# A graph-attention kernel: the last softmax of a layer spread over the next pass, two more products behind the last scores, the bias row on ScalarE

## The chip, the cores and the metric

The kernel runs on one core of a Trainium2 chip. The metric is the device time of one execution in microseconds; the time before is 2698.18 us, the median of three runs (2697.36 to 2700.32). A core has TensorE (PE: matmuls into PSUM banks; PEld is its weight load), VectorE (DVE), ScalarE (ACT), GpSimd (POOL) and SyncE (SP), which issues most of the DMAs. Each runs its own instructions in order and waits on semaphores for the others.

## The reference

Everything is float32. The input is x [128, 64, 768] and a symmetric adjacency of zeros and ones [128, 64, 64] with a full diagonal. After a first normalization there are two layers (l = 0, 1):

```python
h = maximum(layernorm(x), 0)
for l in range(2):
    u_left  = einsum('bih,bjh->bij', h, h @ W_left[l].T)  / sqrt(768)
    u_right = einsum('bih,bjh->bij', h, h @ W_right[l].T) / sqrt(768)
    u = u_left on and above the diagonal, u_right below it (where adj is 1)
    e = exp(u) * adj
    attention = e / (sum(e, axis=2) + 1e-10)
    h = relu(layer_norm(attention @ (h @ W_lin[l].T + b_lin[l])))   # ddof 1, eps added to sigma
x + h
```

## The kernel before, in words

Each layer has two passes. **Pass one** computes the scores and the attention. The 32 parts of 256 tokens are taken in 11 groups (`SUPER`): one of two parts and ten of three. For a group the kernel multiplies weight forms with sums of tokens (a fast matrix multiplication with 40 products, `PRODUCTS`, in place of 54 block products); DVE and ACT read each product out of its PSUM bank and add it into the operands m0, m1, m2 (L847, L851, and L245 for plain additions). The products go round four banks of C, D, X, Y, Z, V. POOL makes the token sums (L245). The scores of a group are 288 small matmuls (L676) into the banks `sc`; they stand four products into the next group. The softmax of a group, a Python generator `chain` (L680 to L715), is cut into eight steps by `yield`: POOL multiplies the two triangles of the adjacency into `wm`; DVE multiplies the scores into `wm` (L690), adds the two halves (L694); ACT takes Exp (L696); DVE masks and sums (L698, L700), divides (L702 to L704), transposes (L708); SP stores the attention with eight DMAs (L713). The steps are put into slots of the next group; a slot is half a product (`put_all`, `turn_of`, `run`), and what a slot holds is issued there on whatever engine it is for.

The last group has no next group. After its 40 products (and the flush of all slots left) come products 0 and 1 of pass two (`LEAD`), then the scores of the last group, then all eight softmax steps in one piece. The adjacency, `wm` and the operands lie in a pool that ends with pass one; its space is used by the tiles of pass two. The 51 places `g` of 128 x 512 elements live through the whole kernel and are handed out and taken back in order through the queue `free`.

During the last group of pass one the plan of `final_of` also loads and prepares what pass two needs: the weights of the linear map (ACT centres them, L233 and L237; DVE and POOL by turns make 17 sums of them), the token sums of its first block (POOL), and the bias row (`bias`, L885 to L913): three DMAs of 256 columns, copied to all partitions, then, on DVE, the sum over the row, the centring, two additions and two negations.

**Pass two** goes over 16 blocks of 512 tokens. `linear` (L1154) does 15 products per block in the order of `ORDER`, each of eight matmuls (L934). Its second entry is the bank by a name that `NAME` maps to the physical bank; `FIRST` tells which products take a fresh bank and `PRELOAD` which of these are first filled with a piece of the bias row by an ACT copy (L923: products 0, 3, 5 and 9). Counted from 0, the banks are 0 in Z, 1 in V, 2 in Z, 3 in X, 4 in Z, 5 in Y, 6 in Z, 7 in X, 8 in Z. The first use of an output piece in `hl` is an ACT activation (L300), later ones are DVE additions (L245); a bank is free for the next product when it is read. Then come the attention times `hl` (L976 or L999), the normalization and the stores.

The order of the work is written by hand: the instructions of an engine stand in the order in which the Python code issues them.

Of the kernel before, what the change touches and what calls it, by code (L numbers as in the profile page):

```python
# [10 lines left out]
F32 = mybir.dt.float32  # L11
I32 = mybir.dt.int32
AF = mybir.ActivationFunctionType
ALU = mybir.AluOpType
# [3 lines left out]
def kernel(  # L18
# [12 lines left out]
    nc = tc.nc  # L31
    B, S, H = x.shape
    L = w_lin.shape[0]
    P = 128
# [35 lines left out]
    def put_all(slot, fs, step=1):  # L70
        for f in fs:
            if f is not None:
                put(slot, f)
            slot += step
        return slot
# [245 lines left out]
    KEEP = {}  # L321
# [299 lines left out]
    def pass_one(l, start, final):  # L621
        with tc.tile_pool(name=f"one{l}", bufs=2, reuse_waits="tile") as sp, \
# [41 lines left out]
                return M[v][:, i * K2:(i + 1) * K2, :, k, :]  # L664

            def scores(k):
                adj, nq = ADJ[k], 2 * len(SUPER[k])
                p = KEEP["scores"].rearrange("p a (q m) -> p (a q) m", m=P)
                for q in range(nq):
                    ht, m = HT[1, l, SUPER[k][q // 2]], M[q // 2]  # L670
                    for c in range(C):
                        for h in range(PAIR):
                            b = q % 2 * PAIR + h
                            mb = m[:, c, b].rearrange("p k j -> p (k j)")
                            for e in (0, 32):
                                nc.tensor.matmul(p[h * S + e:h * S + e + 32, q, e:e + 95],  # L676
                                                 ht[:, c, b * S + e:b * S + e + 32], mb[:, e:e + 95],
                                                 start=(c == 0), stop=(c == C - 1))

                def chain():  # L680

                    wm = sp.tile([P, 6, 2, S], F32, name="wm", bufs=1)[:, :nq]
                    for n in range(2):
                        nc.gpsimd.tensor_tensor(wm[:, :, n], adj[:, :nq, 1 - n],
                                                tri[:, n].unsqueeze(1).to_broadcast([P, nq, S]), op=ALU.mult)
                    yield
                    flat = wm.rearrange("p q k j -> p (q k j)")
                    for i in range(0, P, 32):
                        r = wm.rearrange("p q k j -> p q (k j)")[i:i + 32, :, i % S:i % S + 95]
                        nc.vector.tensor_tensor(r, p[i:i + 32, :nq, i % S:i % S + 95], r, op=ALU.mult)  # L690
                        if i % S:
                            yield
                    v = adj[:, :nq, 0, :]
                    nc.vector.tensor_add(v, wm[:, :, 0], wm[:, :, 1])  # L694
                    yield
                    nc.scalar.activation(v, v, AF.Exp, scale=ISTEMPER if k == 0 else ISTEMPER / 4)  # L696
                    yield
                    nc.vector.tensor_mul(v, v, adj[:, :nq, 1, :])  # L698
                    s = stat.tile([P, 6], F32, name="s", bufs=2)[:, :nq]
                    nc.vector.reduce_sum(s, v, axis=mybir.AxisListType.X)  # L700
                    yield
                    nc.vector.tensor_scalar_add(s, s, EPS_ATT)  # L702
                    nc.vector.reciprocal(s, s)
                    nc.vector.tensor_tensor(v, v, s.unsqueeze(2).to_broadcast([P, nq, S]), op=ALU.mult)  # L704
                    yield

                    at = flat[:, :nq * S].rearrange("p (g q i) -> p g q i", g=2, q=nq)
                    nc.vector.transpose(at.rearrange("p g q i -> p q g i"),  # L708
                                        v.rearrange("p q (g j) -> p q g j", g=2))
                    to = ATT[l][k].rearrange("(b g j) q (h i) -> b h g j q i", b=2, g=2, h=2)  # L710
                    for a in range(4):
                        for g in range(2):
                            nc.sync.dma_start(to[a // 2, a % 2, g], at[a * 32:(a + 1) * 32, g])  # L713

                CHAIN[k] = chain()  # L715

            def softmax(k):
                return [lambda: next(CHAIN[k], None)] * 8

            mid = None  # L720
# [148 lines left out]
            for n in sorted(plan):  # L869
                for f in plan.pop(n):  # L870
                    f()
            for i in range(2):
                LEAD[i] = fresh(l, i, (0, 1))
                multiply(l, 0, i, LEAD[i], (0, 1))
            scores(last)
            for f in softmax(last):
                f()

    rows = {}

# [4 lines left out]
    def bias(l):  # L885


        ab = [free.popleft() for _ in range(2)]
        W[l, "bias"] = ab
        t = rows["bias", l] = [ab[n // 2][:, n % 2, :] for n in range(4)]  # L890
        todo = [lambda i=i, to=to: row(f"b{i}", b_lin[l], i * D, (i + 1) * D, t[to]) for i, to in enumerate((1, 2, 0))]
        bm = stat.tile([P, 3], F32, name="bm", bufs=1)

        bs = stat.tile([P, 1], F32, name="bs", bufs=1)

        def mean():
            for n in range(3):
                nc.vector.reduce_sum(bm[:, n:n + 1], t[n], axis=mybir.AxisListType.X)
            nc.vector.reduce_sum(bs, bm, axis=mybir.AxisListType.X)

        def centred():
            nc.vector.tensor_scalar_mul(bs, bs, -1.0 / H)
            for n in range(3):
                nc.vector.tensor_scalar_add(t[n], t[n], bs)

        def combined():
            nc.vector.tensor_add(t[1], t[1], t[0])
            nc.vector.tensor_add(t[3], t[1], t[2])

        def negated(n):  # L910
            nc.vector.tensor_scalar_mul(t[n], t[n], -1.0)

        return todo, [mean, centred, combined, lambda: negated(0), lambda: negated(2)]  # L913

    AHEAD = []
    PRELOAD = {0: 0, 3: 1, 5: 2, 9: 3}
# [1 line left out]
    def fresh(l, i, rs):  # L918

        bank = ps_st.tile([P, 2 * TH], F32, name=NAME[FIRST[i][0]])  # L920
        b = bank.rearrange("p (r d) -> p r d", r=2)[:, :len(rs)]
        if i in PRELOAD:
            nc.scalar.copy(b, rows["bias", l][PRELOAD[i]].unsqueeze(1).to_broadcast([P, len(rs), D]))  # L923
        return b
# [4 lines left out]
    def multiply(l, u, i, p, rs, between=None):  # L929
        s, _, t, _ = ORDER[i]  # L930
        b, w = tokens_of((2, l, u)), W[l, "n"]
        for n, r in enumerate(rs):
            for c in range(K2):
                nc.tensor.matmul(p[:, n], b[t][:, c, r * P:(r + 1) * P], w[s][:, c, :],  # L934
                                 start=(i in FIRST and i not in PRELOAD and n == c == 0),
                                 stop=(c == K2 - 1), skip_group_check=True)
            if n == 0 and between:
                between()

    def pass_two(l, aside):  # L940
        last = l == L - 1
        with tc.tile_pool(name=f"two{l}", bufs=2, reuse_waits="tile") as sp, \
# [211 lines left out]
            def linear(u, rs, base, ends, more):  # L1154

                if rs[0] == 0:
                    HL[u] = sp.tile([P, Q, H], F32, name="hl", bufs=2)
                hl, seen = HL[u], set()
                bank = {} if LEAD else {"X": AHEAD.pop()}
                early = {0: 3, 2: 5, 6: 9}  # L1160
                for i, (s, at, t, _) in enumerate(ORDER):
                    if i in LEAD:
                        p = bank[at] = LEAD.pop(i)
                        run(base + 2 * i)
                    else:
                        if i in FIRST and i not in PRELOAD:
                            bank[at] = fresh(l, i, rs)
                        p = bank[at]
                        multiply(l, u, i, p, rs, lambda: run(base + 2 * i))
                    read(p, lambda o: hl[:, o % 2 * 2 + rs[0]:o % 2 * 2 + rs[0] + len(rs), o // 2 * D:(o // 2 + 1) * D],  # L1170
                         i, seen, nc.vector if (len(rs), rs[0], i) == (1, 0, 2) and not last else nc.scalar)
                    if i in early:
                        bank[FIRST[early[i]][0]] = fresh(l, early[i], rs)
                    if i == 11 and more and 12 not in ends:
                        AHEAD.append(fresh(l, 0, more))
                    if rs[-1] and t in TS[2, l, u]:
                        free.append(TS[2, l, u].pop(t))
                    if i in ends:
                        what, slots = ends[i]
                        if slots:  # L1180
                            for f, n in zip(finish(*what), slots):
                                put(n, f)
                        else:
                            finish_block(what, more)
                    run(base + 2 * i + 1)
# [100 lines left out]
```

## Time and profile before

| what | value |
|---|---|
| median of the runs | 2698.18 us (2697.36 to 2700.32) |
| profiled execution, whole | 2704.83 us |
| its span from first to last instruction | 2701.9 us |
| mean granted clock of TensorE | 0.988 |
| end of pass one, layer 0 and layer 1 | near 881 to 894 and 2207 to 2219 us |

A line of the timeline has the start in us, the duration, the engine, the source line, the operation, the output and input tiles, their shapes and a count; rows of the same kind that follow each other are merged. In brackets stands how long the engine was idle before it and what released it. "128x512 f32 x3" is three instructions of 128 partitions by 512 elements. PEclk is the granted clock of TensorE as a share of full speed. Ends of matmuls are modelled: a row of eight lasts 1.89 us while the next one starts some 1.73 us after it. SPq and ACTq rows are DMAs being issued. A group line gives the least, the median and the longest duration in ns.

### The profile page before, as it was taken

To read this page: it belongs to the slowest core of one execution; us is meant where nothing else is said; L and a number is where in the kernel's file an instruction comes from. 1 tells how busy PE (TensorE), PEld (TensorE's weight loads), DVE (VectorE), ACT (ScalarE), POOL (GpSimd) and SP (SyncE) were. 2 spreads that over 40 slices of the span, in tenths; PEclk is the share of its full clock that TensorE was granted. 3 is DMA by queue.
4 is the path that set the end of the run, shared out by engine and by line. 5 is a ranking of instruction groups with operands and counts; after the bars stand their busy time and mean duration, and the time that the engine had idled before them with its cause. 6 is when DMAs were issued, how large, how long until landed. Compare 5 with 4: busy or idle time off the path is not lost. (4 is left out here: it accounts for less than half of the span.)

```text
span 2701.9 us, 46786 instructions
## 1 busy us (share of the span) xinstructions
PE 2615.5 (97%) x18042; PEld 2229.1 (83%) x18042; DVE 1765.2 (65%) x2800; ACT 925.8 (34%) x1941; POOL 1725.6 (64%) x1326
## 2 busy tenths in 40 slices
PE   9889999999999899999899999999999979999998
PEld 8778888888887788888678888888888868888886
DVE  7868868776778445554424766776766685666667
ACT  5512222222213144445452212222222315455543
POOL 4756757666667547766215666676666666787786
PEclk9999999999999999999999999999999999999999
DMA  7353443334321344446786443353442105655655
GB/s 215 81 138 80 115 102 92 86 91 123 80 68 62 120 129 155 144 152 205 210 232 181 104 111 86 85 121 91 115 114 68 64 12 156 183 158 159 180 160 149
DMA packets 263358, 336.52 MB, mean 125 GB/s; under 512 B 56290, under 2 KB 195298, under 8 KB 263138
## 3 DMA queue, kind: packets, MB, share of 16 engines
q1 hardware_dynamic: 246338, 325.28, 44.0%
q10 hardware_dynamic: 16800, 8.26, 1.1%
q8 instruction: 144, 2.36, 0.4%
q14 instruction: 76, 0.62, 0.1%
HBM read 218.11 MB, written 115.34 MB: 123 GB/s over the span
## 5 line engine op out<-in xcount | busy, mean ns | idle before, releaser
L245 POOL TENSOR_TENSOR g<-ht 128x512 f32<-128x512 f32 x584 | 769.1, 1327 | 523.6 <-ACT ht L377 135.4
L245 POOL TENSOR_TENSOR g<-g,g 128x512 f32<-128x512 f32 x295 | 378.8, 1292 | 139.9 <-DVE g L245 42.6
L245 POOL TENSOR_TENSOR g<-ht,g 128x512 f32<-128x512 f32 x256 | 339.9, 1335 | 154.7 <-PE X L654 40.3
L934 PE MATMUL Z<-g,g 128*128 128x256 f32 x1024 | 248.5, 385 | 18.3 <-ACT hl L300 9.8
L654 PE MATMUL C<-g,g 128*128 128x256 f32 x1008 | 243.3, 385 | 15.3 <-DVE m L245 7.7
L654 PE MATMUL X<-g,g 128*128 128x256 f32 x1008 | 241.0, 382 | 9.3 <-ACT m L828 4.1
L934 PEld LDWEIGHTS Z<-g,g 128*128 128x128 f32 x1024 | 194.4, 193 | 50.8 <-issue 12.0
L654 PEld LDWEIGHTS C<-g,g 128*128 128x128 f32 x1008 | 191.8, 192 | 46.7 <-POOL g L245 9.4
L654 PEld LDWEIGHTS X<-g,g 128*128 128x128 f32 x1008 | 191.4, 191 | 38.4 <-issue 4.9
L654 PE MATMUL Y<-g,g 128*128 128x256 f32 x912 | 216.5, 380 | 0.0
L654 PE MATMUL D<-g,g 128*128 128x256 f32 x880 | 208.4, 380 | 4.8 <-issue 2.8
L654 PE MATMUL Z<-g,g 128*128 128x256 f32 x864 | 204.7, 380 | 0.0
L377 ACT ACTIVATE ht<-ht,b_col,a_col 128x256 f32<-128x256 f32 x384 | 195.2, 591 | 24.1 <-DMA ht<-h 20.3
L245 DVE TENSOR_TENSOR m<-m,D 128x512 f32<-128x512 f32 x180 | 118.5, 679 | 116.1 <-ACT m L847 98.3
L654 PEld LDWEIGHTS Y<-g,g 128*128 128x128 f32 x912 | 174.2, 191 | 24.0
L654 PEld LDWEIGHTS D<-g,g 128*128 128x128 f32 x880 | 167.0, 190 | 29.1 <-issue 3.7
L934 PE MATMUL X<-g,g 128*128 128x256 f32 x768 | 185.6, 384 | 0.0
L654 PEld LDWEIGHTS Z<-g,g 128*128 128x128 f32 x864 | 163.5, 190 | 23.3 <-issue 0.5
L654 PE MATMUL V<-g,g 128*128 128x256 f32 x768 | 181.4, 379 | 0.0
L934 PEld LDWEIGHTS X<-g,g 128*128 128x128 f32 x768 | 148.3, 193 | 21.5 <-issue 0.6
L245 DVE TENSOR_TENSOR hl<-hl,Y 128x512 f32<-128x512 f32 (+1 forms) x136 | 89.0, 654 | 115.4 <-PE Y L934 96.6
L1134 POOL TENSOR_TENSOR z<-z,b 128x768 f32<-128x768 f32 x62 | 112.6, 1828 | 78.5 <-DVE z L1131 77.2
(215 smaller groups left out, 4728.9 us busy)
## 6 DMA issues: line engine op xcount, KB each, us to landing
ht<-h SPq DMA_DIRECT2D x126, 768.0 KB, 6.4
h<-xb SPq DMA_DIRECT2D x124, 384.0 KB, 5.9
z<-z SPq DMA_DIRECT2D x128, 192.0 KB, 3.1
x<-z SPq DMA_DIRECT2D x128, 192.0 KB, 5.4
xr<-in_x_dram SPq DMA_DIRECT2D x120, 192.0 KB, 3.8
out_dram<-xr SPq DMA_DIRECT2D x120, 192.0 KB, 2.7
x<-in_x_dram SPq DMA_DIRECT2D x112, 192.0 KB, 5.6
g<-form SPq DMA_DIRECT2D x40, 256.0 KB, 5.1
```

The costliest lines, as they stand in the source:

```text
L245: (eng.tensor_add if sign == "+" else eng.tensor_sub)(o, a, b)
L377: nc.scalar.activation(ht, ht, AF.Relu, bias=cols[1][:, c:c + 1], scale=cols[0][:, c:c + 1])
L654: nc.tensor.matmul(p[:, g], w[:, c, g * P:(g + 1) * P], t[:, c, :], start=(new and g == c == 0), stop=(c == K2 - 1), skip_group_check=True)
L934: nc.tensor.matmul(p[:, n], b[t][:, c, r * P:(r + 1) * P], w[s][:, c, :], start=(i in FIRST and i not in PRELOAD and n == c == 0), stop=(c ...
L1134: nc.gpsimd.tensor_add(zs[k], zs[k], rows["b"])
```

## The change

Three things are changed, in both layers.

1. The softmax generator moves out of `scores`, so that it can begin ahead of the scores. For the last group it borrows three places `g` from `free`: one for a copy of the mask (a new POOL instruction), one for the values, one for the transposed result. Nothing of it but `wm`, up to the addition of the two halves, lies in the pool of pass one. Its first step (POOL) is issued ahead of products 0 and 1, the next three (DVE) behind the products that follow the scores, and the last four go into slots 6, 9, 12 and 15 of pass two's first block; then the places go back.
2. Besides products 0 and 1, pass two's products 3 and 5 are issued ahead of pass two: their banks are filled in front of the scores, their matmuls stand behind the scores. `linear` no longer asks for their banks.
3. The bias row's sums (an activation that also gives the sum), its centring and its negations go to ACT; DVE keeps the sum of the three sums, its scaling and the two additions. There are six steps of four slots in place of five.

```diff
             def scores(k):
-                adj, nq = ADJ[k], 2 * len(SUPER[k])
+                nq = 2 * len(SUPER[k])
...
-                CHAIN[k] = chain()
+            def chain(k):
+                adj, nq = ADJ[k], 2 * len(SUPER[k])
+                p = KEEP["scores"].rearrange("p a (q m) -> p (a q) m", m=P)
+
+                spare = [free.popleft() for _ in range(3)] if k == last else ()
+                own = [t.rearrange("p c d -> p (c d)")[:, :nq * S] for t in spare]
...
+                mask = adj[:, :nq, 1, :]
+                if own:
+                    mask = own[0].rearrange("p (q j) -> p q j", q=nq)
+                    nc.gpsimd.tensor_copy(mask, adj[:, :nq, 1, :])
+                yield
...
+                v = own[1].rearrange("p (q j) -> p q j", q=nq) if own else adj[:, :nq, 0, :]
+                nc.vector.tensor_add(v, wm[:, :, 0], wm[:, :, 1])
...
+                nc.vector.tensor_mul(v, v, mask)
...
+                at = (own[2] if own else flat[:, :nq * S]).rearrange("p (g q i) -> p g q i", g=2, q=nq)
...
+                free.extend(spare)
 
             def softmax(k):
+                CHAIN[k] = chain(k)
                 return [lambda: next(CHAIN[k], None)] * 8
...
-            for i in range(2):
+            steps = softmax(last)
+            steps[0]()
+            for i in (0, 1, 3, 5):
                 LEAD[i] = fresh(l, i, (0, 1))
+                if i < 2:
+                    multiply(l, 0, i, LEAD[i], (0, 1))
+            scores(last)
+            for i in (3, 5):
                 multiply(l, 0, i, LEAD[i], (0, 1))
-            scores(last)
-            for f in softmax(last):
+            for f in steps[1:4]:
                 f()
+            put_all(6, steps[4:], 3)
...
+        def sums():
+            for n in range(3):
+                nc.scalar.activation(t[n], t[n], AF.Copy, accum_out=bm[:, n:n + 1])
+
         def mean():
+            nc.vector.reduce_sum(bs, bm, axis=mybir.AxisListType.X)
+            nc.vector.tensor_scalar_mul(bs, bs, -1.0 / H)
+
+        def centred():
             for n in range(3):
-                nc.vector.reduce_sum(bm[:, n:n + 1], t[n], axis=mybir.AxisListType.X)
-            nc.vector.reduce_sum(bs, bm, axis=mybir.AxisListType.X)
-
-        def centred():
-            nc.vector.tensor_scalar_mul(bs, bs, -1.0 / H)
-            for n in range(3):
-                nc.vector.tensor_scalar_add(t[n], t[n], bs)
+                nc.scalar.activation(t[n], t[n], AF.Identity, bias=bs)
...
         def negated(n):
-            nc.vector.tensor_scalar_mul(t[n], t[n], -1.0)
+            nc.scalar.activation(t[n], t[n], AF.Copy, scale=-1.0)
 
-        return todo, [mean, centred, combined, lambda: negated(0), lambda: negated(2)]
+        return todo, [sums, mean, centred, combined, lambda: negated(0), lambda: negated(2)]
...
-                    if i in early:
+                    if i in early and early[i] not in LEAD:
                         bank[FIRST[early[i]][0]] = fresh(l, early[i], rs)
```

More of the change, by code (lines that the diff above doesn't have):

```diff
@@ L678, in scores @@
                                                  start=(c == 0), stop=(c == C - 1))
[L680 to L713, printed above, removed]
@@ L715, in scores @@
-                CHAIN[k] = chain()
+            def chain(k):
[3 more added lines that the diff above has]
+                own = [t.rearrange("p c d -> p (c d)")[:, :nq * S] for t in spare]
+                wm = sp.tile([P, 6, 2, S], F32, name="wm", bufs=1)[:, :nq]
+                for n in range(2):
+                    nc.gpsimd.tensor_tensor(wm[:, :, n], adj[:, :nq, 1 - n],
+                                            tri[:, n].unsqueeze(1).to_broadcast([P, nq, S]), op=ALU.mult)
+                mask = adj[:, :nq, 1, :]
[3 more added lines that the diff above has]
+                yield
+                flat = wm.rearrange("p q k j -> p (q k j)")
+                for i in range(0, P, 32):
+                    r = wm.rearrange("p q k j -> p q (k j)")[i:i + 32, :, i % S:i % S + 95]
+                    nc.vector.tensor_tensor(r, p[i:i + 32, :nq, i % S:i % S + 95], r, op=ALU.mult)
+                    if i % S:
+                        yield
+                v = own[1].rearrange("p (q j) -> p q j", q=nq) if own else adj[:, :nq, 0, :]
+                nc.vector.tensor_add(v, wm[:, :, 0], wm[:, :, 1])
+                yield
+                nc.scalar.activation(v, v, AF.Exp, scale=ISTEMPER if k == 0 else ISTEMPER / 4)
+                yield
+                nc.vector.tensor_mul(v, v, mask)
+                s = stat.tile([P, 6], F32, name="s", bufs=2)[:, :nq]
+                nc.vector.reduce_sum(s, v, axis=mybir.AxisListType.X)
+                yield
+                nc.vector.tensor_scalar_add(s, s, EPS_ATT)
+                nc.vector.reciprocal(s, s)
+                nc.vector.tensor_tensor(v, v, s.unsqueeze(2).to_broadcast([P, nq, S]), op=ALU.mult)
+                yield
+                at = (own[2] if own else flat[:, :nq * S]).rearrange("p (g q i) -> p g q i", g=2, q=nq)
+                nc.vector.transpose(at.rearrange("p g q i -> p q g i"),
+                                    v.rearrange("p q (g j) -> p q g j", g=2))
+                to = ATT[l][k].rearrange("(b g j) q (h i) -> b h g j q i", b=2, g=2, h=2)
+                for a in range(4):
+                    for g in range(2):
+                        nc.sync.dma_start(to[a // 2, a % 2, g], at[a * 32:(a + 1) * 32, g])
+                free.extend(spare)
```

## The prediction

> **What bounds the kernel now.** I read the page first, then the order of time around the two places where pass one hands over to pass two, then the granted clock there, then the waits of TensorE.
>
> ```profile
> span 2701.9 us, 46786 instructions
> PE 2615.5 (97%) x18042; PEld 2229.1 (83%) x18042; DVE 1765.2 (65%) x2800; ACT 925.8 (34%) x1941; POOL 1725.6 (64%) x1326
> ```
>
> TensorE (PE) is busy 97% of the span, so only its holes, and stretches in which it is slow, can be won. The largest hole that the change touches is the end of pass one. This is layer 0, in order of time (start, duration, engine; in brackets the idle time before it and who ended it):
>
> ```profile
> 885.96 6.20 PE L676 MATMUL sc<-m,ht 128*32 128x95 f32 x265 [1.15 <-DVE m L245]
> 893.79 3.03 DVE L690 TENSOR_TENSOR wm<-sc,wm 32x570 f32<-32x570 f32 x4 [4.91 <-issue]
> 896.86 0.56 DVE L694 TENSOR_TENSOR adj<-wm 128x384 f32<-128x384 f32 x1
> 897.45 0.52 ACT L696 ACTIVATE adj<-adj 128x384 f32<-128x384 f32 x1 [20.16 <-DVE adj L694]
> 897.88 0.58 ACT L300 ACTIVATE hl<-Z 128x512 f32<-128x512 f32 x1
> 898.61 3.75 PE L934 MATMUL Z<-g,g 128*128 128x256 f32 x8 [4.92 <-ACT hl L300]
> 902.15 3.12 PE L934 MATMUL X<-g,g 128*128 128x256 f32 x8
> 902.39 0.60 ACT L300 ACTIVATE hl<-Z 128x512 f32<-128x512 f32 x1 [2.93 <-PE Z L934]
> 905.11 1.89 PE L934 MATMUL Z<-g,ht 128*128 128x256 f32 x8
> ...
> 910.29 1.89 PE L934 MATMUL X<-g,g 128*128 128x256 f32 x8
> ```
> ```profile
> core 0: us, PE busy (x) PEld busy (x) DVE busy (x) ACT busy (x) POOL busy (x), PEclk, DMA share, GB/s
> 899.00:902.00 3.00, 3.00 (x8) 2.37 (x8) 2.34 (x6) 0.47 (x1) 0.00 (x0) 0.50 0.02 5
> 906.00:912.00 6.00, 6.00 (x29) 5.30 (x28) 0.76 (x2) 1.68 (x3) 0.33 (x1) 1.00 0.82 265
> ```
>
> The scores end at 893.8, when VectorE (DVE) starts on them. Product 2 of pass two reuses bank Z, whose read stands on ScalarE (ACT) behind the softmax's Exp, and Exp waits for DVE: a hole of 4.92 us. Then products 2 and 3 run at a granted clock of 0.50. Counting the products of pass two as they stand in the kernel's table, the five products 2, 3, 4, 5, 6 lie between 893.79 and the start of product 7 at 910.29: 16.50 us. At full clock a product takes (910.29-905.11)/3 = 1.727 us, five take 8.63; 7.9 us are lost. Layer 1 has the same hole, and the scores of an earlier group show that the scores themselves leave the clock alone:
>
> ```profile
> 2211.71 6.97 PE L676 MATMUL sc<-m,ht 128*32 128x95 f32 x288 [1.15 <-DVE m L245]
> 2223.59 3.75 PE L934 MATMUL Z<-g,g 128*128 128x256 f32 x8 [4.90 <-ACT hl L300]
> ...
> 2234.97 1.89 PE L934 MATMUL X<-g,g 128*128 128x256 f32 x8
> ```
> ```profile
> 809.38 1.47 PE L676 MATMUL sc<-m,ht 128*32 128x95 f32 x58 [0.34 <-issue]
> 810.78 1.99 PE L654 MATMUL C<-g,g 128*128 128x256 f32 x8
> ```
> ```profile
> 2165.99 1.99 PE L654 MATMUL C<-g,g 128*128 128x256 f32 x8 [3.45 <-POOL g L245]
> ```
>
> A product straight behind scores takes 1.99 us, not 3.75, and even 3.45 us of idleness left the next product at 1.99. So it is the 4.9 us hole that halves the clock.
>
> **Part A: two more products behind the scores, the softmax's tail spread.** The instruction order of the changed program shows PE going scores, 3, 5, 2, 4, 6, 7. ACT gets the bias copies for banks X and Y in front of the reads of products 0, 1 and 2; Exp follows the read of 2, the other softmax steps stand between DVE's reads of pass two.
>
> Products 3 and 5 need banks X and Y. DVE's last reads of these lie before 888.9 (it is idle for 4.91 us until 893.79), so both copies are done while the scores run; ACT, idle for 20.16 us there, has the room. The reads of 0 and 1 can run then too. In layer 1 the output tile of these reads lies over the score operands, so they may wait for the scores' end; two reads of 0.6 us are over long before product 2, 3.5 us later. PE therefore goes on at 893.8 without a hole, at full clock.
>
> What is late next: 2, 4 and 6 all use bank Z and now follow each other directly, so PE waits twice for ACT's read of Z. Price from the rows: the read starts 0.03 us after product 2's modelled end (898.61+3.75 = 902.36, read at 902.39), takes 0.60, and PE starts 0.15 us after a read's end (897.88+0.58 to 898.61): 0.78. Rows last 0.16 longer than their spacing, so a turn costs 0.95 us; two cost 1.9. Bounds: nothing, if ACT were ahead, and the clock case below. New stretch: 8.63 + 1.9 = 10.5 us in place of 16.50 in layer 0 (gain 6.0) and of 2234.97-2218.68 = 16.29 in layer 1 (gain 5.8). **Sum 11.7 us.**
>
> Exp now stands in front of ACT's reads of products 4 and 6, and PE waits for those. Its turn comes at 893.8 + 3 x 1.727 + 0.6 = 899.6; DVE's sum of the scores is ready at 896.86+0.56 = 897.42, so there are 2.2 us of slack. On DVE the softmax's 0.55 us steps push its reads of X and Y back by about 1 us; banks X and Y are next written by 7 and by the copy for 9, several products later, so that costs nothing, and 1:1 if those came sooner.
>
> **Part B: the bias row on ScalarE.** In the last group of pass one DVE is behind. PE's rows (first and last of the stretch, and the long waits), DVE's bias row work, and what ACT does then:
>
> ```profile
> 843.04 1.99 PE L654 MATMUL D<-g,g 128*128 128x256 f32 x8 [0.91 <-POOL g L245]
> 845.12 1.07 DVE L898 TENSOR_REDUCE bm<-g 128x1 f32<-128x256 f32 x3 [0.36 <-DMA g<-in_b_lin_dram]
> 848.99 3.72 DVE L904 TENSOR_SCALAR g<-g,bs 128x256 f32<-128x256 f32 x3
> 854.02 1.59 PEld L654 LDWEIGHTS X<-g,g 128*128 128x128 f32 x8 [2.31 <-POOL g L245]
> 854.06 1.97 PE L654 MATMUL X<-g,g 128*128 128x256 f32 x8 [1.93 <-DVE m L245]
> 858.01 1.99 PE L654 MATMUL C<-g,g 128*128 128x256 f32 x8 [0.26 <-DVE m L245]
> 858.59 0.60 ACT L847 ACTIVATE m<-D 128x512 f32<-128x512 f32 x1 [19.25 <-DVE m L851]
> 861.42 1.35 DVE L911 TENSOR_SCALAR g<-g 128x256 f32<-128x256 f32 x1
> 863.42 1.99 PE L654 MATMUL X<-g,g 128*128 128x256 f32 x8 [1.47 <-DVE m L851]
> 865.84 1.27 POOL L245 TENSOR_TENSOR g<-g,g 128x512 f32<-128x512 f32 x1 [3.22 <-DVE g L245]
> 867.30 1.96 PE L654 MATMUL C<-g,g 128*128 128x256 f32 x8
> ```
> ```profile
> 2168.89 1.99 PE L654 MATMUL D<-g,g 128*128 128x256 f32 x8 [0.91 <-POOL g L245]
> ...
> 2193.06 1.97 PE L654 MATMUL C<-g,g 128*128 128x256 f32 x8
> ```
>
> From 843.04 to 867.30 lie eleven products; at 1.727 they take 19.0 us, so 5.3 us are lost (layer 1: 24.17, so 5.2). DVE is rid of 1.07+3.72+1.35 = 6.1 us per layer (and of one short negation), more than the whole loss, so it stops being late. GpSimd (POOL) remains: at 854.02 it released the weights at the same moment as DVE its bank, and it waits 3.22 us for DVE itself. Bounds per layer: 5.3, and 1.7 (0.26+1.47, the waits that are DVE's alone). I take 4.5, near the upper end, because POOL's own longest wait in that stretch is for the same late DVE and goes with it; some tenths stay where POOL is the later one. **Sum 9.0 us.**
>
> ```profile
> L233 ACT ACTIVATE g<-g x36: 399/407/416, 815.0 to 2161.7; 128x256 f32<-128x256 f32 x36
> L233 ACT ACTIVATION_READ_ACCUMULATOR g<-g x36: 186/192/203, 815.3 to 2162.0; 128x1 f32 x36
> L237 ACT ACTIVATE g<-g,wmm x36: 491/494/512, 822.7 to 2166.1; 128x256 f32<-128x256 f32 x36
> 837.00 0.61 ACTq L641 DMA_DIRECT2D adj<-in_adj_dram  x1
> 881.18 1.96 POOL L684 TENSOR_TENSOR wm<-adj,tri 128x384 f32<-128x384 f32 x2
> 911.67 1.27 POOL L245 TENSOR_TENSOR g<-ht 128x512 f32<-128x512 f32 x1 [28.52 <-DMA ht<-h]
> ```
>
> ACT takes on 3 x (0.41+0.19) + 3 x 0.49 + 2 x 0.41 = 4.1 us per layer, inside its 19.25 us of idleness; without that cover 4.1 us would come back. The sums wait for the third row's load (about 845, by DVE's wait on it) and hold ACT's queue; behind them stand the four adjacency loads, now issued near 847 and not at 837. POOL needs them at 881: over 30 us of slack. The row's finish sits one step of four slots later, at slot 60 of about 80.
>
> **Part C: borrowed places and queues.** The mask copy adds one POOL instruction per layer, some 1 us by the 881.18 row (two in 1.96), in front of 28.52 us of idleness: nothing, 1 us without it. Three places are out of the pool until slot 15 and come back at its end. On SP the eight stores of the last softmax move behind the next block's two loads and the two attention loads; those go out sooner, since they need only the scores' end, and POOL, which waited 28.52 us for one, starts sooner. The loads of the block after that stand behind the stores, as before; their users are a block (some 28 us) away. Nothing on PE's path.
>
> **Sum:** 11.7 + 9.0 = 20.7 us off the profiled execution (span 2701.9, 2704.83 with what lies around it, 6.65 above the median 2698.18 of the runs shown). I take the gain to be the same in the undisturbed runs: 2698.2 - 20.7 = **2677.5 us**.
>
> **Rivals.**
> 1. POOL, not DVE, bounds the end of pass one: its weight release at 854.02 speaks for it, its own waits for DVE against. B gives nothing: 2686.5.
> 2. The turns on bank Z hold the clock down: products 2, 4 and 6 go at the halved spacing of 902.15-898.61 = 3.54 instead of 1.727, 5.4 us per layer, A shrinks to 0.8: 2688.4. The 3.45 us row at full clock speaks against it. The Trainium skill's page "TensorE: Matmul & The Clock Gate", section "A second HAM failure mode: psum-queue depth-cycling", says that frequent short pauses of PE between bank groups can make the gate fall and rise again; by that rule this rival is what would happen. No row here shows it.
> 3. The change does not do what it says: products 3 and 5 find X or Y still held, wait for the copies until the softmax is through, and DVE's relief only uncovers POOL: about 2696, within 0.2%. The DVE idle before 893.79 speaks against it.
> 4. Slower: Exp late on ACT. If DVE's sum into a borrowed place had to wait for that place's last reader, Exp would hold ACT's reads of Z, and PE with it, 1:1 beyond the 2.2 us of slack. To end over 5.4 us slower it must be late by 2.2 + (20.7+5.4)/2 = 15.3 us in each layer; at 16 us the time is 2698.2 - 20.7 + 2 x 13.8 = 2705. The places taken are those longest free, which speaks against it.
>
> **How the numbers follow.** 0.2% (5.4 us) is about what a measurement of this kernel can tell from no change. Forecast 0.74, rival 1 0.10, rival 2 0.06, rival 3 0.05, rival 4 0.05. Faster 0.90, within 0.2% 0.05, slower 0.05. Low end: turns free (3.8 more) and all of B (1.5 more): 2672. High end: it takes in rivals 1 and 2: 2689. The forecast's own range, with B between 1.7 and 5.3 per layer, is 2672 to 2683.
>
> **What would show it.** Right: no idle row before the product behind the scores, clock 1.00 there, two waits of about 0.8 us on ACT's read of Z, about 10.5 us from scores' end to product 7; eleven products in some 20 us in the last group; no DVE work on the bias row but the small mean and two additions. Wrong: a halved clock with only short pauses, waits on POOL in place of DVE, Exp starting after 900, or stalls of PE in the second block of pass two.

## The result and the profile after: half of the forecast gain

The changed kernel takes 2687.55 us (median of 8 runs, 2684.21 to 2692.35), the kernel before 2698.86 us beside it (8 runs, 2697.36 to 2706.13). The medians differ by 11.3 us; the ratio of the runs is 0.9961, with an interval of 0.9952 to 0.9970, which is 10.5 us, between 8 and 13. The forecast was 2677.5 us, a gain of 20.7 us. The direction was right. The time lies inside the wide range, 2672 to 2689, which took in two rivals, but outside the forecast's own, 2672 to 2683, and the gain is half of what was worked out.

The first lines of the page after:

```profile
span 2685.4 us, 46818 instructions
PE 2610.8 (97%) x18042; PEld 2225.0 (83%) x18042; DVE 1756.3 (65%) x2784; ACT 933.0 (35%) x1963; POOL 1727.2 (64%) x1328
```

The profiled execution took 2688.04 us, its span is 16.5 us shorter than that of before. Not all of that is the change's: the product into bank D that opens the prediction's stretch stood at 843.04 and now stands at 839.00, so 4.0 us were there before any changed instruction mattered. The same product stood at 840.90 in a run of the kernel before with one added store behind this place (below), so such an offset comes from one execution to the next.

**The end of pass one, layer 1, is as forecast.** The changed kernel's order of time there (columns as before: start, duration, engine, line, operation, count, in brackets the idle time and who ended it):

```profile
2200.65 5.81 PE L676 MATMUL sc<-m,ht 128*32 128x95 f32 x248 [1.15 <-DVE m L245]
...
2204.33 1.83 SPq L366 DMA_DIRECT2D ht<-h  x2
...
2206.75 1.02 PE L676 MATMUL sc<-m,ht 128*32 128x95 f32 x40 [0.29 <-issue]
...
2207.71 1.99 PE L950 MATMUL X<-g,g 128*128 128x256 f32 x8
...
2213.84 1.99 PE L950 MATMUL Z<-g,ht 128*128 128x256 f32 x8 [0.69 <-ACT hl L300]
...
2216.62 1.97 PE L950 MATMUL Z<-g,g 128*128 128x256 f32 x8 [0.78 <-ACT hl L300]
...
2218.42 1.89 PE L950 MATMUL X<-g,g 128*128 128x256 f32 x8
```

Product 3 follows the scores without a hole, at full clock (1.99). Products 4 and 6 wait 0.69 and 0.78 us for bank Z. From product 3 to product 7 it takes 2218.42 - 2207.71 = 10.7 us, where 10.5 were forecast. From the start of the scores to product 7 it was 2234.97 - 2211.71 = 23.26 us and is 17.77: a gain of 5.5.

**Layer 0 gains only 2.4** (24.33 us before, 902.11 - 880.15 = 21.96 after). The order of time and the stretches of the changed kernel:

```profile
880.15 6.20 PE L676 MATMUL sc<-m,ht 128*32 128x95 f32 x265 [1.15 <-DVE m L245]
...
882.96 0.33 SPq L366 DMA_DIRECT2D ht<-h  x1
...
883.38 0.86 SPq L980 DMA_DIRECT2D at<-att  x2
...
889.09 0.69 PE L676 MATMUL sc<-m,ht 128*32 128x95 f32 x23 [2.74 <-issue]
...
889.71 3.03 PE L950 MATMUL X<-g,g 128*128 128x256 f32 x8
...
892.53 2.59 PE L950 MATMUL Y<-g,ht 128*128 128x256 f32 x8
892.96 1.44 DVE L702 TENSOR_TENSOR g<-wm 128x384 f32<-128x384 f32 x1
...
897.38 0.51 ACT L704 ACTIVATE g<-g 128x384 f32<-128x384 f32 x1
...
902.11 1.89 PE L950 MATMUL X<-g,g 128*128 128x256 f32 x8
```
```profile
884.00:886.00 2.00, 2.00 (x109) 2.00 (x104) 0.00 (x0) 0.80 (x2) 0.00 (x0) 1.00 0.87 283
886.00:888.00 2.00, 0.35 (x17) 0.14 (x5) 0.00 (x0) 0.00 (x0) 0.41 (x1) 1.00 0.47 160
...
890.00:892.00 2.00, 2.00 (x7) 1.66 (x7) 1.97 (x3) 0.00 (x0) 1.92 (x3) 0.63 0.03 8
892.00:894.00 2.00, 2.00 (x6) 1.55 (x6) 1.95 (x3) 0.00 (x0) 2.00 (x3) 0.52 0.00 0
```

Ahead of the last 23 small matmuls PE stands still for 2.74 us and waits for nothing that the profile shows ("issue"). In the kernel before the wait at this place was 0.83 us:

```profile
892.99 0.69 PE L676 MATMUL sc<-m,ht 128*32 128x95 f32 x23 [0.83 <-issue]
```

New at that time are three loads of pass two, which the kernel before issued at 905.99 and later, behind the attention stores. The share of the DMA engines (second column from the right) is 0.87 while they move. Then the granted clock (third from the right) falls to 0.63 and 0.52, and products 3 and 5 take 3.03 and 2.59.

**The last group of pass one gains 1.8 us instead of 4.5.** The changed kernel:

```profile
839.00 1.99 PE L654 MATMUL D<-g,g 128*128 128x256 f32 x8 [0.91 <-POOL g L245]
...
848.49 1.74 DVE L245 TENSOR_TENSOR g<-g,g 128x512 f32<-128x512 f32 x1 [2.64 <-POOL g L245]
...
853.77 3.11 POOL L245 TENSOR_TENSOR g<-g,g 128x512 f32<-128x512 f32 x2
854.28 1.48 DVE L923 TENSOR_TENSOR g<-g 128x256 f32<-128x256 f32 x1
855.80 1.37 DVE L924 TENSOR_TENSOR g<-g,g 128x256 f32<-128x256 f32 x1
...
857.09 0.68 DVE L859 SCALAR_TENSOR_TENSOR m<-X,m 128x512 f32<-128x512 f32 x1
...
857.82 1.99 PE L654 MATMUL X<-g,g 128*128 128x256 f32 x8 [2.37 <-DVE m L859]
...
861.50 1.97 PE L654 MATMUL C<-g,g 128*128 128x256 f32 x8
```

The eleven products take 861.50 - 839.00 = 22.50 us (24.26 before). The waits of 1.93, 0.26 and 1.47 are gone, and a new one of 2.37 stands in their place: PE waits for DVE's read of bank X (857.09), in front of which DVE does the two additions of the bias row that it kept. Before that DVE waits 2.64 us for POOL. Layer 1, from the product C ahead of the stretch, goes from 2193.06 - 2165.99 = 27.07 us to 25.40, a gain of 1.7:

```profile
2156.60 3.55 PE L654 MATMUL C<-g,g 128*128 128x256 f32 x8 [3.44 <-POOL g L245]
...
2178.32 1.99 PE L654 MATMUL X<-g,g 128*128 128x256 f32 x8 [2.37 <-DVE m L859]
...
2182.00 1.96 PE L654 MATMUL C<-g,g 128*128 128x256 f32 x8
```

Its first row matters for the clock: the prediction quoted this product after 3.45 us of idleness at 1.99 us; here it stands after 3.44 us and takes 3.55. Counted from the product behind it, the eleven products took 24.17 us and now take 22.06, so some tenths of this layer's gain went into that slow product.

So the trace gives 2.4 + 5.5 at the boundary and 1.8 + 1.7 for the bias row, 11.4 us, which fits the 10.5 of the runs. The theories that the experiments test: the moved loads delay PE's own instructions, and the bias row's additions on DVE, beside POOL, are the new bound of the last group.

### The profile page after: what moved, and what is told of

It is laid out like the page before. It is cut to its first block, busy times and chain, and to the rows that moved or that the text cites. A ratio compares the mean times of both kernels' runs of the same rounds, so it can differ in the third digit from the quotient of the medians.

```text
span 2685.4 us, 46818 instructions
## 1 busy us (share of the span) xinstructions
PE 2610.8 (97%) x18042; PEld 2225.0 (83%) x18042; DVE 1756.3 (65%) x2784; ACT 933.0 (35%) x1963; POOL 1727.2 (64%) x1328
## 3 DMA queue, kind: packets, MB, share of 16 engines
q8 instruction: 144, 2.36, 0.4%
## 5 line engine op out<-in xcount | busy, mean ns | idle before, releaser
L654 PEld LDWEIGHTS V<-g,g 128*128 128x128 f32 x768 | 145.9, 190 | 19.8
```

The source lines that it names most:

```text
L654: nc.tensor.matmul(p[:, g], w[:, c, g * P:(g + 1) * P], t[:, c, :], start=(new and g == c == 0), stop=(c == K2 - 1), skip_group_check=True)
```

## The experiments

Beside the experiments the kernel before was timed on the same chip: 2700.88 us for 1 to 3, 2701.09 us for 5, 6 and the run with a store in 4, and 2697.87 us (one run) for the other two runs of 4. Gains that stand beside a ratio are worked out from it.

**1. The two halves alone.** The first run has the changed order at the boundary, with the bias row left on DVE. The second has the boundary of before, with the bias row on ACT. Both diffs are shortened and against the changed kernel; in the second the softmax generator also goes back into `scores`.

```diff
-        def sums():
-            for n in range(3):
-                nc.scalar.activation(t[n], t[n], AF.Copy, accum_out=bm[:, n:n + 1])
...
+                nc.vector.reduce_sum(bm[:, n:n + 1], t[n], axis=mybir.AxisListType.X)
...
-                nc.scalar.activation(t[n], t[n], AF.Identity, bias=bs)
+                nc.vector.tensor_scalar_add(t[n], t[n], bs)
...
-            nc.scalar.activation(t[n], t[n], AF.Copy, scale=-1.0)
+            nc.vector.tensor_scalar_mul(t[n], t[n], -1.0)
```
```diff
...
-            steps = softmax(last)
-            steps[0]()
-            for i in (0, 1, 3, 5):
+            for i in range(2):
                 LEAD[i] = fresh(l, i, (0, 1))
...
             scores(last)
-            for i in (3, 5):
-                multiply(l, 0, i, LEAD[i], (0, 1))
-            for f in steps[1:4]:
-                f()
-            put_all(6, steps[4:], 3)
+            for f in softmax(last):
+                f()
```

> Parts A and C alone; the bias row stays on VectorE as before. If the gains are separate and the profile of the changed kernel is typical (A took 2.4 us in layer 0 and 5.5 us in layer 1), this is 8 us faster than before, ratio 0.997. If A gives what was predicted in both layers it is 11.7 us, 0.9957. If the layer 0 hole in the scores (2.74 us, put down to issue) comes from the block loads that now go out during the scores, it stands here too, between 2 and 3 us. If it was chance, it is back near the 0.83 us of before.

> Part B alone; the end of pass one as before. By the profile of the changed kernel B is worth 1.8 and 2.1 us: 3.9 us, ratio 0.9986. If the prediction's size was right it would be 9.0 us, 0.9967. In the trace the eleven products of the last group take about 22.3 us again (24.2 before, 19.0 without a wait), with one wait of 2.4 us of TensorE for VectorE's reads of bank X in each layer.

The boundary alone takes 2692.83 us, ratio 0.9973 (0.9962 to 0.9983), a gain of 7.3 us. The bias row alone takes 2697.0 us, ratio 0.9989 (0.9980 to 0.9998), a gain of 3.0 us. Together that is 10.3, the gain of the whole change: within these intervals the halves add up, and both are smaller than forecast (11.7 and 9.0). The bias row alone, at the place of the new wait:

```profile
860.82 1.99 PE L654 MATMUL X<-g,g 128*128 128x256 f32 x8 [2.38 <-DVE m L851]
```

The wait of 2.4 us belongs to the bias row; in layer 1 of this run it is 1.32, not the 2.4 that was expected in each layer, because PE came to it late, behind products at a lower clock (3.78 us). The issue wait belongs to the boundary: 2.28 us in the first run, 0.82 in the second.

**2. The additions later.** The two additions and the negations go to slots 64 to 68, behind the reads that PE waits for.

```diff
-                put_all(slot + 40, work, 4)
+                for n, f in zip((40, 44, 48, 64, 66, 68), work):
+                    put(slot + n, f)
```

> The changed kernel, but the two additions of the bias row and the negations behind them move from slots 52, 56, 60 to 64, 66, 68 of the last group. If the additions (2.85 us on VectorE there) are what holds the reads of bank X, the 2.37 us wait of TensorE disappears in both layers and it is up to 4.7 us faster than the changed kernel, unless they hold something else at their new place. If VectorE is late because of its own wait for GpSimd (2.64 us at 848.5), the wait of TensorE stays above 1.5 us and the time is within 1.5 us of the changed kernel.

Measured 2685.45 us, ratio 0.9938 (0.9925 to 0.9950). This interval lies below that of the changed kernel (0.9952 to 0.9970): some 6 us faster, a little more than the 4.7 at most that were expected. The trace of this run:

```profile
838.90 1.99 PE L654 MATMUL D<-g,g 128*128 128x256 f32 x8 [0.91 <-POOL g L245]
...
848.38 1.74 DVE L245 TENSOR_TENSOR g<-g,g 128x512 f32<-128x512 f32 x1 [2.57 <-POOL g L245]
...
855.18 1.89 PE L654 MATMUL X<-g,g 128*128 128x256 f32 x8
...
858.63 1.92 PE L654 MATMUL C<-g,g 128*128 128x256 f32 x8
```

The wait ahead of X is gone, and the eleven products take 19.73 us, where 19.0 is the time without waits. DVE's wait for POOL is still there (2.57), so POOL did not bound PE: the place of the additions did. In layer 1 the stretch from C takes 22.90 us (2155.05 to 2177.95) in place of 25.40. The two layers gain 2.8 + 2.5 = 5.3 us in the trace; with that the bias row is worth 8.7, close to the forecast 9.0.

**3. The loads held back.** The loads of the second block from h now depend on a one-column write by DVE that stands behind its reads of the scores; the attention loads wait behind them on SP.

```diff
-                    load_h(2, l, u + 1)
+                    if u:
+                        load_h(2, l, u + 1)
+                    else:
+                        for t in range(2):
+                            ht = HT[2, l, 2 + t] = big.tile([P, C, TH], F32, name="ht", bufs=6)
+                            paced(ht[:, 0, :1], lambda ht=ht, t=t: nc.sync.dma_start(ht, KEPT[l][2 + t]))
```

> The changed kernel, but the two loads of pass two's second block are held by a VectorE write of one column that stands behind the scores' reads. If those loads starve TensorE's instruction fetch in the scores of layer 0, the issue wait there falls from 2.74 to below 1 us, the products behind the scores run at full clock (about 1.73 us apart in place of 2.8 and 2.4), and it is 3 to 4 us faster than the changed kernel. If the hole has another cause it stays and the time is that of the changed kernel within 1 us.

Its trace, the end of pass one in layer 0 and the place of the wait for bank X in layer 1:

```profile
877.35 6.38 PE L676 MATMUL sc<-m,ht 128*32 128x95 f32 x265 [1.15 <-DVE m L245]
884.64 0.69 PE L676 MATMUL sc<-m,ht 128*32 128x95 f32 x23 [0.91 <-issue]
885.26 2.00 PE L950 MATMUL X<-g,g 128*128 128x256 f32 x8
...
895.97 1.89 PE L950 MATMUL X<-g,g 128*128 128x256 f32 x8
...
2174.59 3.62 PE L654 MATMUL X<-g,g 128*128 128x256 f32 x8 [2.39 <-DVE m L859]
```

The issue wait is back at 0.91, the clock holds, and from the scores' start to product 7 it takes 18.62 us: 5.7 less than before, where 6.0 were forecast. In the trace the boundary's steps were right; the loads were what they left out. The runs do not show it: 2689.65 us, ratio 0.9958 (0.9945 to 0.9972), where 3 to 4 us under the changed kernel (0.9961) were expected. The intervals are wide enough to hide such a gain, so the time neither confirms nor refutes it. The last row shows one thing that differs between executions: here the 2.39 us wait lowered the clock (3.62), which it did not do in the changed kernel's first profile; but in its second profile (experiment 5) it did (3.38 behind 2.36), so this does not explain the missing gain. Why the runs gained less than the trace stays open.

**4. Which load, and how.** Three runs put different transfers into the last scores of layer 0: the changed kernel with only the attention loads held, the same with only the loads from h held, and the kernel before with an added store of 768 KB from a score operand to an unused place in DRAM (the first two diffs are against the changed kernel, the third against the kernel before, where the store is work on top).

```diff
-                    nc.sync.dma_start(AT[u][:, 2 * t:2 * t + 2], ATT[l][k][:, 2 * i:2 * i + 2])
+                    go = lambda t=t, k=k, i=i: nc.sync.dma_start(AT[u][:, 2 * t:2 * t + 2], ATT[l][k][:, 2 * i:2 * i + 2])
+                    paced(AT[u][:, 2 * t, :1], go) if u == 0 else go()
```
```diff
-                put(4, lambda u=u: load_at(u))
+                if u:
+                    put(4, lambda u=u: load_at(u))
                 if u + 1 < NB:
-                    load_h(2, l, u + 1)
+                    if u:
+                        load_h(2, l, u + 1)
+                    else:
+                        load_at(0)
+                        for t in range(2):
+                            ht = HT[2, l, 2 + t] = big.tile([P, C, TH], F32, name="ht", bufs=6)
+                            paced(ht[:, 0, :1], lambda ht=ht, t=t: nc.sync.dma_start(ht, KEPT[l][2 + t]))
```
```diff
+            away = dram.tile([P, C * T], F32, name=f"away_{l}")
+            nc.sync.dma_start(away[:, :C * TH], M[0].rearrange("p c b k s -> p (c b k s)")[:, :C * TH])
             scores(last)
```

> The changed kernel with the two loads of attention values of the first block (64 KB each, 256 bytes at a time) held until VectorE has read the last scores; the load of 768 KB from h still goes out while the scores run. If it is the many small packets of the attention loads that delay PE's instructions, the issue wait in layer 0's last scores falls from 2.7 to 0.9 us or less. If it is the load of 768 KB, it stays over 2 us.

> The reverse of the run beside it: the two attention loads go out while the scores run, the loads from h are held until VectorE has read the last scores. If the small packets are the cause, the issue wait stays over 2 us; if the load of 768 KB is, it falls to 0.9 us or less. If both falls are seen, neither load is enough alone.

> The kernel before with one added store of 768 KB from one of the score operands to an unused place in DRAM, issued on SP while the last scores run; nothing on PE depends on it. If it is the transfer as such that delays PE's instructions, the issue wait in the middle of the last scores (0.83 us before) becomes 2 to 3 us in layer 0, with no load of pass two moved. If it is something else in the moved loads (their queue, their place, the product order), the wait stays at 0.8 us.

Whole times of one run each: 2683.41, 2688.78 and 2702.84 us. Eight runs of the changed kernel spread over 8 us, so these single times say little; the traces are what counts here. The DMA view of the changed kernel for 886.5 to 887.5 us has a queue named "instruction" beside the data queue; in the kernel before, that view shows nothing else between 880 and 898 us:

```profile
q1 hardware_dynamic: 204, 0.13, 41.1%
q8 instruction: 1, 0.02, 5.5%
```
```profile
DMA packets 2, 0.03 MB, mean 2 GB/s; under 512 B 0, under 2 KB 0, under 8 KB 0
...
q8 instruction: 2, 0.03, 0.7%
```

Cut into windows of 0.05 us, this view gives the time of the last such packet ahead of the wait. Counted from the first of the last scores in layer 0:

| kernel | in flight during the scores | packet goes at | PE goes on after the packet | issue waits, together |
|---|---|---|---|---|
| before | nothing | 4.3 us | 2.7 us | 0.83 us |
| loads held (3) | nothing | 4.7 us | 2.6 us | 0.91 us |
| only attention loads | 2 x 64 KB | 5.3 us | 2.3 us | 1.19 us |
| before with a store | 768 KB out | 5.0 us | 2.7 us | 1.29 us |
| only the load from h | 768 KB in | 6.5 us | 2.2 us | 2.39 us |
| changed | 768 KB in, 2 x 64 KB | 6.7 us | 2.2 us | 2.74 us |

In these rows PE goes on 2.2 to 2.7 us after a 16 KB packet of this queue, and the packet goes some 2 us later when the load from h is in flight. The load of 768 KB is enough, the small packets are not; with them alone the wait was 1.19 us, a little over the 0.9 that was expected. That the packet carries PE's next instructions is read from the queue's name and this timing; the profile does not say it outright. The store missed its expectation of 2 to 3 us. It was issued 0.6 us after the scores' start (884.38 against 883.81) and nearly all its bytes were through by 887.0, before the packet went at 888.8. The load in the run that held the attention loads was issued 2.8 us after the scores' start; it kept the DMA share at 0.79 to 0.84 from 881 to 884 us, and the packet went at 884.05, as it ended. So the run does not tell a store from a load, it only shows that a transfer which is over in time costs little. Layer 1 of the changed kernel fits: there the packet went at 2204.0, the loads were issued from 2204.33, and the issue wait was 0.29.

The kernel before already shows the wait, at places that nobody changed. In layer 0 the scores of four groups run beside transfers that fill the DMA engines (the view prints a share of 1.04 to 1.05 from 1 to 6 us after their start) and wait 2.15 to 3.06 us on issue. Of the other 18 groups of both layers, with a share of 0.56 or less, 17 wait 0.86 us or less and one waits 2.30 us, at a share of 0.50, which stays unexplained. One of the four:

```profile
655.15 3.78 PE L676 MATMUL sc<-m,ht 128*32 128x95 f32 x95 [3.06 <-issue]
```

**5. One turn less.** Product 5 goes behind product 2, so that products 2 and 4 no longer follow each other on bank Z.

```diff
-            for i in (3, 5):
-                multiply(l, 0, i, LEAD[i], (0, 1))
+            multiply(l, 0, 3, LEAD[3], (0, 1))
...
+            put(5, lambda p=LEAD[5]: multiply(l, 0, 5, p, (0, 1)))
```

> The changed kernel with product 5 behind product 2 instead of ahead of it, so that products 2 and 4 no longer follow each other on bank Z: one turn on Z is left per layer instead of two. If a turn costs 0.95 us, product 7 starts 0.95 us sooner in each layer, together 1.9 us (0.07%) under the changed kernel. If the turns were hidden behind something else, nothing changes. If Z's read for product 2, now later behind the scores, is the later one, product 2 waits and the time rises.

> The changed kernel itself, for comparison beside the next two on one chip: some 10 us (0.4%) under the kernel before. If the 12 us from product 3 to product 7 in layer 0 come from loads that overtake the scores, a long issue wait of PE of over 2 us stands again in the middle of the last scores of layer 0, and none in layer 1.

2687.19 us (ratio 0.9956, 0.9943 to 0.9968), beside 2690.18 us of the changed kernel (0.9966, 0.9955 to 0.9978): the expected 1.9 us lie within the intervals and are not told apart by the time. The trace shows them. In layer 1 of the new kernel product 3 starts at 2207.16 and product 7 at 2216.92, 9.76 us in place of 10.71: one turn costs 0.95, as the prediction priced it. In layer 0 the scores' start to product 7 takes 21.00 us in place of 21.96. The changed kernel's second trace, layer 0:

```profile
890.68 0.69 PE L676 MATMUL sc<-m,ht 128*32 128x95 f32 x23 [2.83 <-issue]
891.30 2.00 PE L950 MATMUL X<-g,g 128*128 128x256 f32 x8
```

The issue wait is there again, but this time the clock stays up behind it, and from the scores' start to product 7 it takes 20.54 us.

**6. All three mends.**

> Three mends of the changed kernel at once: the loads of the second block held until the scores are read, the two additions and the two negations of the bias row put 24 slots later, product 5 behind product 2. Worked out from the single ones: 10.5 us of the change, 2.0 to 3.5 for the additions, 1.7 to 3 for the loads, 1.9 for the turn: 16 to 19 us under the kernel before, ratio 0.993 to 0.994. If the mended holes only move elsewhere, it stays at the changed kernel's 10 us.

The diffs of 2, 3 and 5 together take 2678.07 us (2674.81 to 2681.78, 5 runs), ratio 0.9918 (0.9905 to 0.9931): 22 us faster than before, where 16 to 19 were expected, and 12 us faster than the changed kernel on the same chip. The best kernel of this study. Its trace:

```profile
836.31 2.00 PE L654 MATMUL D<-g,g 128*128 128x256 f32 x8 [0.91 <-POOL g L245]
...
856.05 1.91 PE L654 MATMUL C<-g,g 128*128 128x256 f32 x8
...
874.83 6.20 PE L676 MATMUL sc<-m,ht 128*32 128x95 f32 x265 [1.15 <-DVE m L245]
...
881.63 0.69 PE L676 MATMUL sc<-m,ht 128*32 128x95 f32 x23 [0.60 <-issue]
...
892.01 1.89 PE L950 MATMUL X<-g,g 128*128 128x256 f32 x8
```

Eleven products in 19.74 us, 17.18 us from the scores' start to product 7 (24.33 before), with one turn. By the traces that is 4.5 + 7.2 us in layer 0 and 4.4 + 6.2 in layer 1 (22.66 us from C, 17.08 us from the scores), 22.3 together, which is what the runs gained. The time lies near the forecast of 2677.5, but only with three changes that the forecast did not have.

## Why the prediction was right and wrong

**Part A, layer 1: right.** No hole behind the scores, clock 1.00, turns of 0.69 and 0.78, Exp in time: 5.5 us for the forecast 5.8. The price of a turn, 0.95, was confirmed by experiment 5. In layer 0 Exp started at 897.38, straight behind the read of product 2 and 3.0 us after DVE's sum was ready, so rival 4 did not come.

**Part A, layer 0: short by 3.6 us, and the failing step stands in part C.** That step followed the loads as far as POOL ("those go out sooner"), gained from that, and closed with "Nothing on PE's path". It did not ask what else uses the DMA engines while a transfer that was behind the stores now runs during 288 small matmuls. PE's issue wait rose from 0.83 to 2.74, and in the profiled execution the clock fell behind it. In the second execution, where the clock stayed up, the layer gained 3.8, so about 2 us of the shortfall are the wait and the rest the clock. With the loads held it gained 5.7 in the trace. The price could be read in the kernel before, at the four groups of experiment 4.

**Part B: right in direction, wrong in size, 3.5 us for 9.0.** The failing step is "so it stops being late", and with it "I take 4.5, near the upper end". The 6.1 us that DVE was rid of were counted at the durations they had beside POOL: the negation (L911) takes 1.35 us at 861.42, while POOL works, and 0.28 at 865.68, while it does not. A part of the 6.1 was thus waiting, and waiting came back: DVE waits 2.64 us for POOL, and the two additions that stayed on DVE were given no price. They take 1.48 and 1.37 us beside POOL and stand ahead of the read that PE needs. That the measured 1.8 and 1.7 equal the lower bound of the prediction is chance: the bound took two waits to go, but three went and a new one of 2.37 came. The negation in the kernel before, with POOL idle (the prediction shows its longer one):

```profile
865.68 0.28 DVE L911 TENSOR_SCALAR g<-g 128x256 f32<-128x256 f32 x1
```

The later additions of experiment 2 bring 2.8 and 2.5 of the missing time. Rival 1 named POOL as the bound; that is half right, since POOL stretched and delayed DVE, but its own releases did not hold PE: with the additions moved, PE ran within 0.7 us of its pace although DVE still waited 2.57 for POOL. The measured time lies between those of rival 1 (2686.5) and rival 2 (2688.4), but neither of them happened; two other shortfalls add up to nearly the same.

**Rival 2: not seen in its form, but its subject was.** Turns of 0.69 and 0.78 us, two to a layer, never lowered the clock in any trace here. A clock did fall, behind longer holes. The argument against the rival, one row at 1.99 after 3.45 us, was too weak to be a rule: behind the same wait of 3.44 us on POOL that product took 2.00, 2.52, 2.96, 3.55 and 3.78 us in five of the kernels (loads held, additions later, all mends, changed, bias row alone).

**The small terms held.** PE never waited for ACT's added work, the mask copy on POOL took 0.51 us, and the adjacency loads went out at 842.5, where 847 was expected. The gain of the one pair of executions was no measure of the runs, though: 16.5 us between the spans, 10.5 by the ratio of the runs.

## What to carry to other kernels

When a change moves work on a queue, ask what starts to overlap with the moved transfers, the instruction stream of the busy engine included: a load that is issued early can cost more than it saves if it runs beside many small matmuls. When an engine is rid of work, look at what remains of that work and what stands behind it on the same engine, at the durations it has beside its neighbours; a duration that a neighbour has stretched is not all relief. A clock state read off one row is one sample: look for the same hole in several executions before arguing with it.

## What the runs showed of the hardware that was not expected

**The clock falls at a chance moment.** After holes of 4.90 and 4.92 us the next product took 3.75 us, in the kernel before and in the two runs that keep these holes. After 3.44 us it took anything from 1.99 to 3.78, and behind the issue waits of 2.74 and 2.83 us, in two executions of one kernel, 3.03 and 2.00. The wait for bank X in the last group, 2.15 to 2.39 us long, stands thirteen times in the traces: eight times the product took 1.99 or 2.00, four times 3.38 to 3.68, and once 2.47 with 3.15 for the next one. The Trainium skill, page "TensorE: Matmul & The Clock Gate", section "What's actually happening", says that the clock has two states, full and half, that the half state comes after at least one idle window of about 3.4 us, and that the windows run freely, so that the moment of the switch varies from run to run. The two speeds (clock 0.50 to 0.52 and 1.00) and the varying outcome agree with it; the holes of 2.15 to 2.39 us behind which the clock fell are shorter than that window, and there the measurement decides.

**An addition on DVE takes over three times as long beside POOL.** The bias row's addition of 128x256 took 1.48 us (L923) beside a running POOL addition. In the kernel before the first of the two additions began while POOL was idle, the second while POOL was at work:

```profile
855.54 0.41 DVE L907 TENSOR_TENSOR g<-g 128x256 f32<-128x256 f32 x1
...
855.69 1.38 POOL L245 TENSOR_TENSOR g<-g,g 128x512 f32<-128x512 f32 x1 [0.63 <-DVE g L245]
...
855.99 1.37 DVE L908 TENSOR_TENSOR g<-g,g 128x256 f32<-128x256 f32 x1
```

The Trainium skill, page "SBUF — State Buffer", section "SBUF: two separate sides", says that DVE and GpSimd share one pair of ports: a DVE operation with two inputs in SBUF and a GpSimd operation that reads SBUF cannot hold it together, and the one that comes second waits for the whole length of the first. The rows agree: 0.41 us for the addition that came first, and the second addition, begun at 855.99, ends at 857.36, 0.29 us after the POOL instruction (857.07).
